# V's second third product between the two banks of scores, the gather in one run, and V's last wide products cut in halves

## The chip, the cores and the metric

The kernel runs on one core of a Trainium2 chip. The metric is the device time of one execution in microseconds (us), the median of several runs. A core has a matrix engine (TensorE, "PE" in the profile, with its weight loads shown apart as "PEld"), a vector engine (DVE), an activation engine (ACT), GpSimd (POOL) and a queue engine for transfers (SP). Matrix products end in PSUM, which has eight banks of 128 x 512 numbers; everything else lies in SBUF.

## The reference, cut to what matters

`x` has 64 graphs of 256 nodes with 512 features; `adj` is 256 x 256 with zeros and ones. Two layers follow each other:

```python
h = relu(layernorm(x))
q, k, v = h @ Wq.T, h @ Wk.T, h @ Wv.T
rel = adj.T * (q @ k.T)                       # scores, per graph
rel = rel / norm(rel, axis=2, keepdims=True)
x = x + rel @ v
h = relu(layernorm(x))
x = x + (adj @ h) @ weight + bias
```

All is float32.

## The kernel before

**Precision by thirds.** A float32 operand is split into three parts, named `u`, `l` and `s` (upper, lower, and one for the cross terms), and a product is the sum of three: u with u, l with l, s with s. Between the second and the third, ACT multiplies the PSUM bank by a constant just over one (line 361). `three` makes these products for one bank: `first(ps)` gives u and l, `second(ps)` the third one. `unit` plans a bank: it takes the next of eight banks, plans `first`, then plans what the unit before has left over in the list `waiting` (its third product and its `drain`), then ACT's multiplication, and puts its own rest into `waiting`. So a unit's third product stands on PE behind the next unit's first two, which hides ACT's multiplication. `finish` plans whatever is in `waiting`.

**Stages.** Two graphs make a pair; there are 32 pairs, numbered from 0. For a pair i, the loop in `pairs` plans:

- `g_stage`: four banks of g = M h, with M = Wq and Wk multiplied once at the start. A third is 4 matmuls of 512 columns (weights `m_*`, moving `h_*` or `hs`). The drain splits g into `gy_u`, `gy_s`, `gy_l` (lines 265, 266, 268).
- `v_stage` for block 0 and for block 1: V = h Wv for 128 nodes each, 4 + 4 + 4 matmuls of 512 columns (tiles `wv_*`, `h_*`, `hs`). The drain writes three rows of `late` (tiles `v_low`, `late_parts`). Block 1's drain is held back in the list `held` until the gather is planned, since it writes over rows that the gather reads.
- `scores`: two banks, one for each graph. A third is 8 matmuls of 256 columns (weights `gy_*`, moving `h_*` or `hs`). The drain multiplies by the adjacency on DVE (line 444) and takes sums of squares on ACT (line 449).
- `gather` of pair i - 1: adj times h of layer 2, four banks of 8 matmuls of 256 columns (weights `late`, moving `adjt_r`). It has no third product, so it plans what is in `waiting` behind its first bank. Its drain splits the result into the same `gy_*` rooms, for `mix` (lines 274 to 276).
- `turn_scores`, `v_stage` for blocks 2 and 3, the turn of the next pair's h (`h_turn`, `h_parts`), `mix` of pair i - 1 (tiles `w_*`, `gy_*`), `attend` of pair i (tiles `v_low`, `late_parts`, `rel_*`), and with its last block `layer_1`, which makes the rows that the next gather reads.

Pair 0 has scores but no gather; in the last pair the gather of that pair follows at the end.

**Order.** The class `Plan` takes the operations with costs and with what they read and write. PE keeps the order in which it was planned. The other engines and queues are ordered by due times, which come from PE's order and from the costs; each engine then runs its list strictly in order. All matmuls are recorded at line 255, in the helper `mm`.

On PE, an ordinary pair around the scores is therefore: V block 0's third product; u and l of the first bank of scores; V block 1's third product; u and l of the second bank; third product of the first bank; first bank of the gather; third product of the second bank; the other three banks of the gather; V blocks 2 and 3.

Of the kernel before, what the change touches and what calls it, by code (L numbers as in the profile page):

```python
# [108 lines left out]
def f(ap):  # L109
    return ap.bitcast(F32)  # L110
# [3 lines left out]
def kernel(  # L114
# [13 lines left out]
    B, N, D = x.shape  # L128
    DC = D // P
    NC = N // P  # L130
# [7 lines left out]
    outs = out.rearrange("(i b) (c p) d -> i p (b c) d", b=NB, p=P)  # L138
# [4 lines left out]
    def room(name, *shape, dtype=F32, tag=None):  # L143
        return pool.tile([P, *shape], dtype, name=name, tag=tag or name)
# [11 lines left out]
    def hp(k, d):  # L156
        return h[k][:, d] if k < 2 else h_s[d // 2][:, d % 2]
# [43 lines left out]
    def late(r):  # L201

        return v_low[:, r] if r < 4 else changing("late", "parts", 8, D, dtype=F32R)[:, r - 4]
# [16 lines left out]
    def by_pe(i):  # L220

        return i < 2 or i + 1 == NP
# [17 lines left out]
    def next_bank(turned=False, on=None):  # L240

        while on is not None and count["bank"] % 8 in in_pieces:
            count["bank"] += 1
        n = count["bank"] % 8
        count["bank"] += 1
        (in_pieces.add if turned else in_pieces.discard)(n)
        return bank[n], ("bank", n)
# [3 lines left out]
    def keys(name, n=DC):  # L251
        return [(name, k) for k in range(n)]

    def mm(out, left, right, first):
        nc.tensor.matmul(out, left, right, start=first, stop=True, skip_group_check=True)  # L255

    MM, HALF = 0.231, 0.1185
# [85 lines left out]
    waiting = []  # L343

    def finish(plan):
        while waiting:
            waiting.pop(0)()

    def unit(plan, first, second, drain, on=None):


        ps, key = next_bank(on=on)
        if on is not None:
            plan.add("ACT", 0.58, lambda: A.copy(ps, on), ["bias"], [key])
        for cost, fn, reads in first(ps):
            plan.add("PE", cost, fn, reads, [key])
        finish(plan)
        if second is None:
            drain(ps, key)
            return  # L360
        plan.add("ACT", 0.49, lambda: A.activation(ps, ps, AF.Copy, scale=ONE), [], [key])  # L361

        def rest():
            for cost, fn, reads in second(ps):
                plan.add("PE", cost, fn, reads, [key])
            drain(ps, key)
        waiting.append(rest)

    def three(left, right, names_l, names_r, cost, outs=None, fresh_bank=True):


        def group(k, ds, begin):
            def first(ps):
                for d in ds:
                    for n, (o, lf, rt) in enumerate(outs(ps, k, d) if outs else [(ps, left(k, d), right(k, d))]):
                        mm(o, lf, rt, begin and d == ds[0] and n == 0)
            return first

        def first(ps):
            for k, ds, begin in ((0, (0, 1), fresh_bank), (0, (2, 3), False), (1, (0, 1, 2, 3), False)):  # L380
                yield cost * len(ds), (lambda go=group(k, ds, begin): go(ps)), [
                    n for d in ds for n in (*names_l(k, d), *names_r(k, d))]

        def second(ps):
            ds = (0, 1, 2, 3)
            yield cost * len(ds), (lambda go=group(2, ds, False): go(ps)), [
                n for d in ds for n in (*names_l(2, d), *names_r(2, d))]
        return first, second

    def named(*names):  # L390
        return lambda k, d: [(names[k], d)]
# [4 lines left out]
    def g_half(b):  # L396

        return lambda k, d: [(name + "uls"[k], d, b) for name in ("gy_", "g_")]
# [4 lines left out]
    h_named = named("h_u", "h_l", "h_s")  # L403
# [12 lines left out]
    def v_stage(plan, i, exact, blocks_of=range(4), hold=False):  # L416
        for c in blocks_of:
            first, second = three(
                lambda k, d, c=c: hp(k, d)[:, ts(c, P)], lambda k, d: wv_p[k][:, d, :],
                h_named, named("wv_u", "wv_l", "wv_s"), MM)  # L420
            rows = [[("late", 3 * c + k)] for k in range(3)]
            if c == 1 and not exact:
                rows[2] = keys("late", 12)[4:]

            def drain(ps, key, c=c, rows=rows):
                split_right_ps(plan, ps, key, [lambda at, k=k: late(3 * c + k) for k in range(3)], rows, None)
            unit(plan, first, second, (lambda ps, key, go=drain: held.append(lambda: go(ps, key))) if hold else drain)

    def scores(plan, i):
        rn = norms[i % 2]  # L430
        for b in range(NB):
            def outs_of(ps, k, d, b=b):
                return [
                    (ps[:, ts(n, N)], g_p[k][:, d, ts(b * NC + n, P)], hp(k, d)[:, ts(b, N)])
                    for n in range(NC)
                ]
            first, second = three(None, None, g_half(b), h_named, 2 * HALF, outs_of)

            def drain(ps, key, b=b):
                dst = plain[:, b].rearrange("p k (t j s) -> p k t j s", t=NC, j=J) if by_pe(i) else rel[:, b]  # L440

                def columns(part):
                    return part.rearrange("p (k t j s) -> p k t j s", k=NC, t=NC, j=J)
                plan.add("DVE", 0.6, lambda: V.tensor_mul(
                    *(part.rearrange("p k t j s -> p (k t) j s") for part in (
                        dst, columns(ps), columns(f(adjt[0]).rearrange("p k m -> p (k m)")))),),
                    [key, "adjt"], [("h_rel", b)])
                for k in range(NC):
                    plan.add("ACT", 0.53, lambda k=k: A.activation(
                        columns(ps)[:, k], dst[:, k], AF.Square, accum_out=rn[:, b, k : k + 1]),  # L450
                        [("h_rel", b)], [key, (f"rn{i % 2}", b, k)])
            unit(plan, first, second, drain)

    def turn_scores(plan, i):
        rn, name = norms[i % 2], f"rn{i % 2}"
# [249 lines left out]
    def pairs(exact):  # L705
        count["bank"] = 4
        waiting.clear()
        rooms.clear()
        plan = Plan()
        turned_adj = room("adjt_r", NC * N + P, dtype=F32R, tag="adjt") if exact else room("adjt", NC * N + P)  # L710
        adjt[:] = [turned_adj[:, P - 16 : P - 16 + NC * N].rearrange("p (c n) -> p c n", c=NC)]
        plan.add("ACT", 0.49, lambda: A.copy(adjt[0].rearrange("p m n -> p (m n)"), bank[6]), [("bank", 6)], ["adjt"])
        first_turn(plan)
        last_m(plan)
        count["bank"] = 4
        turn_wv(plan)
        h_rows(plan, 1)
        h_place(plan, 25.0)
        load(plan, 2)
        first_g(plan)  # L720
        v_stage(plan, 0, exact, (0, 1))
        scores(plan, 0)
        v_stage(plan, 0, exact, (2, 3))
        turn_scores(plan, 0)
        finish(plan)
        h_turn(plan)
        h_parts(plan)
        split_w(plan)
        plan.add("ACT", 0.58, lambda: A.activation(bias_bc, bias_bc, AF.Copy, scale=1.0 / ONE), [], ["bias"])
        attend(plan, 0, exact)  # L730
        for i in range(1, NP):
            last = i + 1 == NP
            load(plan, i, name=f"x{i % 2}")
            if not last:
                h_rows(plan, i + 1)
                h_place(plan)
            if i + 2 < NP:
                load(plan, i + 2)
            g_stage(plan, i)
            v_stage(plan, i, exact, (0,))  # L740
            v_stage(plan, i, exact, (1,), hold=True)
            scores(plan, i)
            gather(plan, i - 1, exact)
            while held:
                held.pop(0)()
            if by_pe(i):
                turn_scores(plan, i)
            v_stage(plan, i, exact, (2, 3))
            if not last:
                if not by_pe(i):  # L750
                    turn_scores(plan, i)
                waiting.append(lambda: (h_turn(plan), h_parts(plan)))
                mix(plan, i - 1)
            attend(plan, i, exact)
            if last:
                mix(plan, i - 1)
                gather(plan, i, exact)
            store(plan, i - 1)
        mix(plan, NP - 1)
        finish(plan)  # L760
        with tc.manual_schedule(engines=in_order):
            plan.run()
# [33 lines left out]
```

## Time and profile before

| What | Value |
| --- | --- |
| Median of 3 runs (lowest, highest) | 1561.76 us (1561.21, 1562.63) |
| The profiled execution's own time | 1560.76 us |
| Its span in the profile | 1559.0 us |
| PE, weight loads, DVE, ACT busy | 99%, 85%, 87%, 66% |
| Granted TensorE clock | 0.999 |
| Matmuls recorded | 8046 |
| Moved from and to HBM | 67 GB/s over the span |

The span is the time from the first to the last instruction of the profiled execution; its own time has 1.8 us more around it. A row of the timeline gives the start, the time until the end of the last one, engine, line, operation, the tiles as out<-in, the shape and how many instructions were merged. Matmuls overlap in it, so the pace of a run is read from the start of one row to the start of the next.

### The profile page before, as it was taken

To read this page: it belongs to the slowest core of one execution; us is meant where nothing else is said; L and a number is where in the kernel's file an instruction comes from. 1 tells how busy PE (TensorE), PEld (TensorE's weight loads), DVE (VectorE), ACT (ScalarE), POOL (GpSimd) and SP (SyncE) were. 2 spreads that over 40 slices of the span, in tenths; PEclk is the share of its full clock that TensorE was granted. 3 is DMA by queue.
4 is the path that set the end of the run, shared out by engine and by line. 5 is a ranking of instruction groups with operands and counts; after the bars stand their busy time and mean duration, and the time that the engine had idled before them with its cause. 6 is when DMAs were issued, how large, how long until landed. Compare 5 with 4: busy or idle time off the path is not lost.

```text
span 1559.0 us, 22543 instructions
## 1 busy us (share of the span) xinstructions
PE 1548.2 (99%) x8046; PEld 1323.5 (85%) x8046; DVE 1355.3 (87%) x2419; ACT 1022.7 (66%) x1941; POOL 24.3 (2%) x39
## 2 busy tenths in 40 slices
PE   9999999999999999999999999999999999999998
PEld 6788888888888888888888888888888888888886
DVE  6997889898889988898988899888989888989786
ACT  5567666666667676666676675766666766666654
POOL 0000000000000000000000000000000000000000
PEclk9999999999999999999999999999999999999999
DMA  5321333223333223333233332233332233322211
GB/s 199 112 83 41 122 111 120 77 71 110 118 113 119 66 78 117 114 117 90 72 96 118 112 122 68 77 114 114 116 106 71 81 121 111 120 71 76 85 55 56
DMA packets 91112, 153.63 MB, mean 99 GB/s; under 512 B 17136, under 2 KB 32240, under 8 KB 90992
## 3 DMA queue, kind: packets, MB, share of 16 engines
q1 hardware_dynamic: 80768, 116.46, 24.7%
q0 software_dynamic: 8432, 32.51, 5.7%
q10 hardware_dynamic: 1792, 3.15, 0.6%
q8 instruction: 65, 1.06, 0.3%
q14 instruction: 55, 0.45, 0.1%
HBM read 70.78 MB, written 33.55 MB: 67 GB/s over the span
## 4 chain that ended last, share of the span: by engine, by line
PE 95%; DVE 3%; DMA 1%; ACT 0%; issue 0%; ACTq 0%; DVEq 0%
PE bank L255 95%; DMA bias_bc<-in_L_gnn_bias_dram 1%; DMA x_ring<-in_x_dram 1%; DVE late_parts L266 0%; DVE late_parts L268 0%; DVE rel_s_parts L470 0%; DVE st L292 0%; DVE rel_l L475 0%; DVE gy_l L275 0%; DVE m_l L268 0%; DVE gy_l L268 0%; DVE wv_l L268 0%; DVE ht L322 0%; DVE wv_s L266 0%; DVE m_s L266 0%
## 5 line engine op out<-in xcount | busy, mean ns | idle before, releaser
L361 ACT ACTIVATE bank<-bank 128x512 f32<-128x512 f32 x572 | 333.5, 583 | 307.8 <-PE bank L255 304.2
L255 PE MATMUL bank<-wv_s,hs 128*128 128x512 f32 x512 | 137.8, 391 | 0.0
L255 PE MATMUL bank<-wv_u,h_u 128*128 128x512 f32 x512 | 137.5, 390 | 0.0
L255 PE MATMUL bank<-wv_l,h_l 128*128 128x512 f32 x512 | 136.9, 389 | 0.0
L255 PE MATMUL bank<-w_u,gy_u 128*128 128x512 f32 x512 | 136.9, 389 | 0.0
L255 PE MATMUL bank<-w_l,gy_l 128*128 128x512 f32 x512 | 136.9, 389 | 0.0
L255 PE MATMUL bank<-h_l,m_l 128*128 128x512 f32 x512 | 136.6, 389 | 0.1
L255 PE MATMUL bank<-w_s,gy_s 128*128 128x512 f32 x512 | 136.7, 389 | 0.0
L255 PE MATMUL bank<-h_u,m_u 128*128 128x512 f32 x512 | 136.5, 389 | 0.0
L255 PE MATMUL bank<-hs,m_s 128*128 128x512 f32 x512 | 136.4, 389 | 0.0
L266 DVE SCALAR_TENSOR_TENSOR gy_s<-gy_u,bank 128x512 fp32r<-128x512 f32 x128 | 86.2, 675 | 43.0 <-ACT gy_u L265 43.0
L255 PEld LDWEIGHTS bank<-h_l,m_l 128*128 128x128 f32 x512 | 96.0, 188 | 20.4 <-DVE h_l L339 0.5
L255 PEld LDWEIGHTS bank<-wv_l,h_l 128*128 128x128 f32 x512 | 96.1, 188 | 20.2
L255 PEld LDWEIGHTS bank<-h_u,m_u 128*128 128x128 f32 x512 | 96.0, 188 | 20.2 <-ACT m_u L265 0.2
L255 PEld LDWEIGHTS bank<-w_l,gy_l 128*128 128x128 f32 x512 | 96.1, 188 | 20.0
L255 PEld LDWEIGHTS bank<-hs,m_s 128*128 128x128 f32 x512 | 96.1, 188 | 19.9
L255 PEld LDWEIGHTS bank<-w_u,gy_u 128*128 128x128 f32 x512 | 96.0, 188 | 20.0
L255 PEld LDWEIGHTS bank<-w_s,gy_s 128*128 128x128 f32 x512 | 96.0, 188 | 20.0 <-ACT bank L361 0.2
L255 PE MATMUL bank<-adjt_r,late_parts 128*128 128x256 f32 x896 | 112.6, 277 | 0.0
L255 PEld LDWEIGHTS bank<-wv_s,hs 128*128 128x128 f32 x512 | 93.8, 188 | 18.3 <-ACT bank L361 0.7
L255 PEld LDWEIGHTS bank<-wv_u,h_u 128*128 128x128 f32 x512 | 93.7, 188 | 17.7
L255 PEld LDWEIGHTS bank<-adjt_r,late_parts 128*128 128x128 f32 x896 | 107.3, 188 | 0.0
(110 smaller groups left out, 3072.3 us busy)
## 6 DMA issues: line engine op xcount, KB each, us to landing
fresh<-in_x_dram SPq DMA_DIRECT2D x31, 1024.0 KB, 5.7
blocks<-h_rel SPq DMA_DIRECT2D x496, 64.0 KB, 2.0
x_ring<-in_x_dram SPq DMA_DIRECT2D x31, 1024.0 KB, 8.0
out_dram<-x_ring POOLq DMA_DIRECT2D x31, 1024.0 KB, 5.4
h_rel<-h_rel SPq DMA_DIRECT2D x464, 32.0 KB, 1.8
blocks<-in_L_gnn_Wv_dram ACTq DMA_DIRECT2D x1, 1024.0 KB, 11.1
x_ring<-in_L_gnn_weight_dram SPq DMA_DIRECT2D x1, 1024.0 KB, 12.3
out_dram<-x_ring SPq DMA_DIRECT2D x4, 256.0 KB, 2.3
```

The source lines that it names most:

```text
L255: nc.tensor.matmul(out, left, right, start=first, stop=True, skip_group_check=True)
L266: plan.add("DVE", 0.63, lambda: V.scalar_tensor_tensor(s(), f(u()), ONE, ps, op0=ALU.mult, op1=ALU.subtract), [*key, *ku], ks)
L361: plan.add("ACT", 0.49, lambda: A.activation(ps, ps, AF.Copy, scale=ONE), [], [key])
```

## The change

Three things change in the order and shape of PE's work.

1. `three` gets a flag `halve`. With it, the last matmul of the third product (k = 2, d = 3, the last chunk of the contraction) is given as two matmuls of 256 columns with the same weights. `v_stage` sets it for blocks 0 and 1, in every pair.
2. `scores` takes a function `between`. It is called after both banks' units are planned; the loop hands it what `waiting` held, that is V block 1's third product with its drain. Taken out of `waiting`, that product no longer stands behind u and l of the first bank.
3. After `between`, `scores` calls `finish`, so that the second bank's third product is planned at once, and not behind the first bank of the gather.

PE's order in pairs 1 to 31 becomes: V block 0's third product; u and l of the first bank of scores; u and l of the second; third product of the first bank; V block 1's third product; third product of the second bank; all four banks of the gather. Pair 0 calls `scores` without `between`: there only the halves are new, and no `finish` is called. The order of SP's and POOL's transfers stays as it was; on DVE and ACT some operations of a pair change places, by the planner's due times.

```diff
-    def three(left, right, names_l, names_r, cost, outs=None, fresh_bank=True):
+    def three(left, right, names_l, names_r, cost, outs=None, fresh_bank=True, halve=False):
...
                 for d in ds:
-                    for n, (o, lf, rt) in enumerate(outs(ps, k, d) if outs else [(ps, left(k, d), right(k, d))]):
+                    whole = outs(ps, k, d) if outs else [(ps, left(k, d), right(k, d))]
+                    if halve and k == 2 and d == DC - 1:
+                        whole = [(o[:, ts(n, N)], lf, rt[:, ts(n, N)]) for o, lf, rt in whole for n in range(NC)]
+                    for n, (o, lf, rt) in enumerate(whole):
                         mm(o, lf, rt, begin and d == ds[0] and n == 0)
...
-                h_named, named("wv_u", "wv_l", "wv_s"), MM)
+                h_named, named("wv_u", "wv_l", "wv_s"), MM, halve=c < NC)
...
-    def scores(plan, i):
+    def scores(plan, i, between=None):
...
             unit(plan, first, second, drain)
+        if between:
+            between()
+            finish(plan)
...
-            scores(plan, i)
+            scores(plan, i, waiting.pop())
             gather(plan, i - 1, exact)
```

## The prediction

> **What bounds the kernel.** First the page's busy shares, then its chain, then the waits of PE.
>
> ```profile
> PE 1548.2 (99%) x8046; PEld 1323.5 (85%) x8046; DVE 1355.3 (87%) x2419; ACT 1022.7 (66%) x1941; POOL 24.3 (2%) x39
> ...
> PE 95%; DVE 3%; DMA 1%; ACT 0%; issue 0%; ACTq 0%; DVEq 0%
> ```
>
> ```profile
> PE bank L255 <- DVE rel_s_parts L470: 1.2, 1, 1.2
> PE bank L255 <- DMA wk_sb<-in_L_gnn_Wk_dram: 1.1, 1, 1.1
> PE bank L255 <- POOL h_rel L612: 1.0, 1, 1.0
> PE bank L255 <- DVE late_parts L268: 0.7, 1, 0.7
> PE bank L255 <- DVE rel_l L475: 0.6, 1, 0.6
> ```
>
> PE is busy for 99% of the span, the chain that ends last is 95% PE, and all waits of PE listed come to 4.6 us, each happening once (start, first pair, last pair). Its weight loads (PEld) were held for ACT bank L361 six times, 2.9 us in all. In an ordinary pair between, no engine and no transfer holds PE up. So the time is the number of matmuls times their pace, and the view that counts is the PE timeline, read from start to start (rows overlap, so the durations in the second column cannot be added). An ordinary pair:
>
> ```profile
> 174.32 1.07 PE L255 MATMUL bank<-wv_s,hs 128*128 128x512 f32 x4
> 175.23 1.10 PE L255 MATMUL bank<-h_u,gy_u 128*128 128x256 f32 x8
> 176.17 1.11 PE L255 MATMUL bank<-h_l,gy_l 128*128 128x256 f32 x8
> 177.12 1.09 PE L255 MATMUL bank<-wv_s,hs 128*128 128x512 f32 x4
> 178.04 1.11 PE L255 MATMUL bank<-h_u,gy_u 128*128 128x256 f32 x8
> 178.99 1.10 PE L255 MATMUL bank<-h_l,gy_l 128*128 128x256 f32 x8
> 179.93 1.11 PE L255 MATMUL bank<-hs,gy_s 128*128 128x256 f32 x8
> 180.87 0.40 PE L255 MATMUL bank<-adjt_r,v_low 128*128 128x256 f32 x2
> 181.11 0.85 PE L255 MATMUL bank<-adjt_r,late_parts 128*128 128x256 f32 x6
> 181.80 1.10 PE L255 MATMUL bank<-hs,gy_s 128*128 128x256 f32 x8
> 182.74 0.40 PE L255 MATMUL bank<-adjt_r,v_low 128*128 128x256 f32 x2
> 182.98 2.66 PE L255 MATMUL bank<-adjt_r,late_parts 128*128 128x256 f32 x22
> 185.47 1.08 PE L255 MATMUL bank<-wv_u,h_u 128*128 128x512 f32 x4
> ```
>
> Scores (gy) from 178.04 to 180.87: 24 matmuls in 2.83 us, **117.9 ns** each. Gather (adjt_r) from 182.98 to 185.47: 22 in 2.49, **113.2 ns** each, for the same shape. Two products of 512 columns take 2 x 226.7 elsewhere (24 of w between 712.76 and 718.20), so 113.3 is half of a wide one and 117.9 is 4.5 ns too slow. Now an odd pair, in which PE's weight load had been held for 0.19 us by ACT at 126.74:
>
> ```profile
> 129.67 1.09 PE L255 MATMUL bank<-wv_s,hs 128*128 128x512 f32 x4
> 130.60 1.07 PE L255 MATMUL bank<-h_u,gy_u 128*128 128x256 f32 x8
> 131.50 1.07 PE L255 MATMUL bank<-h_l,gy_l 128*128 128x256 f32 x8
> 132.41 1.07 PE L255 MATMUL bank<-hs,gy_s 128*128 128x256 f32 x8
> 133.32 0.40 PE L255 MATMUL bank<-adjt_r,v_low 128*128 128x256 f32 x2
> ```
>
> The same scores: 24 in 2.72 us, 113.3 ns. Then the gather of that pair is slow (135.42 to 138.01: 22 in 2.59, 117.7 ns). So a 256-column run has **two paces**, set by how it is entered and kept through the run; four wide products between do not change it (fast on both sides of 129.67); after slow scores the gather is fast, after fast scores it is slow. The stall at 798.49 switched the scores in the same way. Straight from undisturbed wide products the scores always come in slow. Why is not told by the trace.
>
> **What the Trainium skill says.** "TensorE: Matmul & The Clock Gate", section Back-to-back issue gap: the spacing in a stream of weight loads and matmuls is set by both, and its table gives 262 cycles at 256 columns and 518 at 512. That prices a product cut in two at 6 cycles, an estimate of 2.5 ns at the page's 2.4 GHz; the trace has neither figure (113.3 or 117.9, and 226.7), and its bounds are 0 to 9 ns (2 x 113.3 or 2 x 117.9 less 226.7). "Perfetto Trace Analysis", section Identifying the Most-Contended Engine: matmul busy time misleads, weight-load busy is the better measure; here that is 85%, which agrees that something is left, and the pace above says where. "SBUF — State Buffer", section Who interferes with whom: moving operand and weights have a read port each and PE waits on nobody. No run here shows a cause that contradicts it, but two paces with no wait do exist.
>
> **The change, part by part.** The stretch from the first score to the first wide product after the gather takes 185.47 - 175.23 = 10.24 us (10.24 also at 744.49 to 754.73), in 31 pairs. It holds 48 + 32 narrow matmuls and 4 wide ones: at 113.3 and 226.7 that is 9.97. So **0.27 us per pair** can be won at most: 48 x 4.5 ns = 0.22 in the scores, the rest at the changes of kind.
> - *Halves.* The last wide matmul of V's third product becomes two narrow ones, for blocks 0 and 1 in all 32 pairs: 64 more matmuls and weight loads. Direct price 0 to 9 ns each; I take 5, +0.01 us per pair. Their indirect effect is that the scores are no longer entered straight from a wide product. Trace before shows no such entry; bounds: nothing, or 40 scores (all before the second V third) from 117.9 to 113.3, -0.18 us.
> - *V's third moved.* It now stands after the third products of bank 0 and before those of bank 1. Number and operands are unchanged. In before it costs 178.04 - 177.12 = 0.92 against 0.907, and something alike stays. With its own halved last product it can switch the pace once more. I take it that it does: the last 8 scores slow (8 x 4.5 = 0.04 us that stays), and the gather fast as it is now after slow scores. Bounds: gather unchanged, or 32 x 4.5 = +0.14 us.
> - *Gather in one run.* One entry into it less: 182.74 to 185.47 is 24 matmuls in 2.73 against 2.72, and 180.87 to 181.80 is 8 in 0.93 against 0.907; -0.02 us per pair.
> - *What moves on the other engines.* SP and POOL issue the same DMAs in the same order. Bank 0's scores end about 0.9 us earlier, bank 1's about 1 us, so mask, squares and the later DMA turn start earlier; the first gather ends 0.9 us later, the last where it did. Costed at nothing, with this cover: gy_l for bank 0, last written at 744.27 + 0.69 = 744.96, is read last from 746.1; gy_s, ready at 744.26, would be read from about 748.2 instead of 749.2. V's block 1 leaves PE about 2.7 us later; its DVE work on the bank ran at 753.96, the next V product into that bank comes at 756.34, and one gather part of 0.68 us now goes ahead on DVE: some 1.7 us of slack left after 0.68 of work become 1.0. On ACT its copy must follow the second gather anyway, which ends where it did. Later in the pair DVE does the turn of the scores before h's second half and h_l after rel_s; rel_l, now 0.8 us ahead of its first use (769.81 against 770.62), gets more room, and h_l still ends near 772.2 for a use at 776.96. If a cover went, the late one would be V's bank at 756.34, at tenths of a us per pair.
>
> Sum per pair: -0.18 - 0.02 + 0.02 = -0.18 us, times 31 = -5.6; the first pair, which has scores and no gather, -0.1. The profiled execution took 1560.76 us (span 1559.0 and 1.8 around it), so it would come to 1555.1; the median shown is 1.0 above it: 1556.1.
>
> **The rivals.**
> - *All fast* (8%): scores and gather both near 113.3, up to -0.27 x 31 = -8: 1553.5. For it: both paces exist for both kinds. Against it: in no pair of before were both fast throughout.
> - *One switch only* (12%): the first third switches the scores, the second does not; 48 fast scores (-0.22) and 32 slow gathers (+0.14), with the rest -0.06 to -0.09: 1559 to 1560. For it: this is what the pair at 130.60 looks like.
> - *No switch* (16%): the halves are just two more matmuls, +0.01 to +0.02, and the single run of gather returns 0.02: 1561 to 1562.5. This is also the case that the change does not do what it can do.
> - *The gather turns slow and the scores stay slow* (14%): the switch happens only at the second halved third. 40 scores slow, 8 fast (-0.04), 32 gathers at 117.7 (+0.14), halves and entries 0 to +0.02: +0.10 to +0.14, +3.2 to +4.3 in all: about 1565.5. It decides as soon as fewer than 32 of the 48 scores gain their pace while the gather loses its own. Against it: the first entry changes more than the second, which comes in among narrow runs anyway.
>
> **Numbers.** Likeliest, 50%: 1556.1, its own range 1554.5 to 1557.5. A measurement of this kernel can tell about 0.2%, 3.1 us, from no change: faster means below 1558.6. The likeliest, all fast and a part of one switch: 66% faster. The other part and no switch: 20% within. Slower: 14%. The range runs from all fast to no switch, 1553.3 to 1562.6, and leaves out the slower case and little else.
>
> **What would show it.** Right: eight h_u,gy_u matmuls start to start 0.91 us instead of 0.94, in nearly all pairs; the gather's 32 still 3.63 to 3.66; the stretch 10.06 instead of 10.24; PE's waits unchanged. Wrong: scores at 0.94 still; or a gather run of 3.77; or a new repeated wait of PE for DVE late_parts or ACT bank L361.

## The result, and the profile after

The change makes the kernel slower: 1565.56 us (median of 10 runs, 1564.34 to 1566.6) against 1561.85 (10 runs, 1560.27 to 1562.77). The ratio is 1.0023, with a 95% interval of 1.0014 to 1.0032. The profiled execution took 1565.42 us, its span is 1563.6, so 4.6 us over the span before.

The page's busy shares and the chain of the changed kernel; below them, the waits of PE's weight loads between 100 and 1500 us (in total, times, longest), first of the kernel before, then of the changed one:

```profile
PE 1550.4 (99%) x8110; PEld 1327.3 (85%) x8110; DVE 1359.4 (87%) x2419; ACT 1020.7 (65%) x1941; POOL 24.3 (2%) x39
...
PE 85%; DVE 5%; ACT 3%; SPq 3%; DMA 1%; issue 1%; DVEq 0%; ACTq 0%
```

```profile
PEld bank L255 <- ACT bank L361: 0.7, 3, 0.4
```

```profile
PEld bank L255 <- ACT bank L361: 3.2, 6, 0.8
PEld bank L255 <- DVE late_parts L266: 0.4, 1, 0.4
```

PE has the 64 matmuls more, and the chain leaves PE for 15% of the span instead of 5%: something now comes late for PE, which nearly nothing did before. But first the PE timeline of an ordinary pair (columns as before; the row of five wv_s is three wide matmuls and the two halves):

```profile
744.73 1.08 PE L255 MATMUL bank<-wv_s,hs 128*128 128x512 f32 x5
745.64 1.11 PE L255 MATMUL bank<-h_u,gy_u 128*128 128x256 f32 x8
746.59 1.10 PE L255 MATMUL bank<-h_l,gy_l 128*128 128x256 f32 x8
747.53 1.11 PE L255 MATMUL bank<-h_u,gy_u 128*128 128x256 f32 x8
748.47 1.10 PE L255 MATMUL bank<-h_l,gy_l 128*128 128x256 f32 x8
749.41 1.11 PE L255 MATMUL bank<-hs,gy_s 128*128 128x256 f32 x8
750.36 1.09 PE L255 MATMUL bank<-wv_s,hs 128*128 128x512 f32 x5
751.29 1.07 PE L255 MATMUL bank<-hs,gy_s 128*128 128x256 f32 x8
752.20 0.40 PE L255 MATMUL bank<-adjt_r,v_low 128*128 128x256 f32 x2
752.43 0.87 PE L255 MATMUL bank<-adjt_r,late_parts 128*128 128x256 f32 x6
753.14 0.40 PE L255 MATMUL bank<-adjt_r,v_low 128*128 128x256 f32 x2
753.38 2.75 PE L255 MATMUL bank<-adjt_r,late_parts 128*128 128x256 f32 x22
755.97 1.09 PE L255 MATMUL bank<-wv_u,h_u 128*128 128x512 f32 x4
```

From 745.64 to 750.36 stand 40 scores in 4.72 us, 118.0 ns each: the cut product at 744.73 switched nothing. From 751.29 to 752.20 stand 8 in 0.91, 113.8 ns: the cut product at 750.36 did switch. And the gather that comes in behind fast scores is slow, 32 in 3.77 us (752.20 to 755.97), 117.8 ns. The stretch is 10.33 us where before had 10.24; read to the ns over the trace's starts it is 10.325 against 10.246 in nearly every pair, and 0.079 x 31 = 2.4 us. The rest of the 4.6 lies in four pairs between 1126 and 1319 us: their periods, from first score to first score, are 48.15, 47.93, 48.40 and 48.09 us, where 47.53 is the rule. That is 2.45 us together; the start and the end give back some tenths. (A fifth long pair, at 793 us with 47.82, is no loss: before has it too, with 47.90.)

So three theories for the experiments. **A**: a cut V product makes a run of narrow matmuls fast only where it stands inside such a run, and the gather behind fast scores is slow. Rival **B**: the new order itself makes the gather slow. **C**, on the rest of the loss: the long pairs begin with a late load of `fresh`. Each time below stands beside that of the kernel before, run again on the same chip.

### The profile page after: what moved, and what is told of

Same layout as the page of the kernel before. It is cut to its first block, busy times and chain, and to the rows that moved or that the text cites. A ratio compares the mean times of both kernels' runs of the same rounds, so it can differ in the third digit from the quotient of the medians.

```text
span 1563.6 us, 22615 instructions
## 1 busy us (share of the span) xinstructions
PE 1550.4 (99%) x8110; PEld 1327.3 (85%) x8110; DVE 1359.4 (87%) x2419; ACT 1020.7 (65%) x1941; POOL 24.3 (2%) x39
## 4 chain that ended last, share of the span: by engine, by line
PE 85%; DVE 5%; ACT 3%; SPq 3%; DMA 1%; issue 1%; DVEq 0%; ACTq 0%
PE bank L255 85%; SPq L231 3%; DMA fresh<-in_x_dram 1%; DVE st L292 1%; ACT h_rel L306 1%; ACT bank L454 0%; ACT bank L354 0%; ACT gy_u L274 0%; DVE h_rel L449 0%; ACT bank L361 0%; DVE ht L322 0%; DVE late_parts L266 0%; DVE gy_l L268 0%; DVE rel_s_raw L492 0%; DVE gy_s L266 0%
## 5 line engine op out<-in xcount | busy, mean ns | idle before, releaser
L361 ACT ACTIVATE bank<-bank 128x512 f32<-128x512 f32 x572 | 332.7, 582 | 349.1 <-PE bank L255 349.1
L255 PE MATMUL bank<-wv_s,hs 128*128 128x512 f32 (+1 forms) x576 | 138.6, 367 | 0.9 <-ACT bank L361 0.8
L275 DVE TENSOR_TENSOR gy_l<-bank,gy_u 128x512 fp32r<-128x512 f32 x128 | 85.2, 685 | 53.7 <-ACT gy_u L274 53.7
L255 PEld LDWEIGHTS bank<-wv_s,hs 128*128 128x128 f32 x576 | 105.5, 188 | 23.2 <-ACT bank L361 3.2
L255 PE MATMUL bank<-adjt_r,late_parts 128*128 128x256 f32 x896 | 116.0, 281 | 0.0
```

Of the source, the lines that this page charges most:

```text
L275: plan.add("DVE", 0.6, lambda: V.tensor_sub(l, ps, f(u)), [key, *ku], kl)
```

## The experiments

**move_only: the order alone, no cut.**

```diff
-                h_named, named("wv_u", "wv_l", "wv_s"), MM, halve=c < NC)
+                h_named, named("wv_u", "wv_l", "wv_s"), MM, halve=False)
```

> The changed order (V block 1's third product between the two banks' third products, the gather in one run), with no product cut in halves. Theory A (a cut product inside a narrow run switches the pace): all 48 scores stay at 117.8 ns, V's four wide ones take about 0.926 us, the gather's 32 start within 0.02 us to run at 113.3; the stretch from the first score to the first wide product after the gather is about 10.23 us (before 10.246, after 10.325), the time 0 to 1 us below before. Rival B (the order itself, a gather straight behind a bank's third product, makes the gather slow): gather at 117.8, stretch 10.32 or more, 2 us or more above before.

The end of the stretch in its PE timeline:

```profile
1037.75 1.11 PE L255 MATMUL bank<-hs,gy_s 128*128 128x256 f32 x8
1038.69 0.40 PE L255 MATMUL bank<-adjt_r,v_low 128*128 128x256 f32 x2
...
1039.84 2.66 PE L255 MATMUL bank<-adjt_r,late_parts 128*128 128x256 f32 x22
1042.33 0.86 PE L255 MATMUL bank<-wv_u,h_u 128*128 128x512 f32 x3
```

Scores slow (0.94 for 8), gather fast: 22 in 2.49, 113.2 ns; the stretch 10.225. That is A's figure, and B falls: the order does not slow the gather. But the time was 1564.27 (21 runs) against 1561.92, ratio 1.0014 (1.0007 to 1.0020), where A expected a gain. In the profile the loss stands in long pairs, six of them by 0.4 to 1.0 us, and in weight loads held by ACT L361 for 4.8 us in 9 waits. The order brings the long pairs, without any cut.

In one of these long pairs a hold of PE at 461.6 us had made the scores fast ahead of V's whole product. What came behind it:

```profile
463.64 1.07 PE L255 MATMUL bank<-hs,gy_s 128*128 128x256 f32 x8
464.55 1.09 PE L255 MATMUL bank<-wv_s,hs 128*128 128x512 f32 x4
465.48 1.11 PE L255 MATMUL bank<-hs,gy_s 128*128 128x256 f32 x8
466.42 0.40 PE L255 MATMUL bank<-adjt_r,v_low 128*128 128x256 f32 x2
```

Eight in 0.91, then eight in 0.94: here the pace fell behind four wide products. In before, at 129.67 us, the scores kept the fast pace behind four wide ones, and the prediction took that one case for the rule.

**halves_only: the order of before, both cuts.**

```diff
-            scores(plan, i, waiting.pop())
+            scores(plan, i)
```

> The order of before, with the last wide product of V's third cut in halves for blocks 0 and 1. Theory A: the first bank's 16 scores slow; behind the cut V product the 16 of the second bank and the 8 third ones fast (113.3 ns); the gather's first 8 slow (117.8), the 8 scores behind them fast, the gather's other 24 slow; stretch 10.22 to 10.26 us, the time within 1 us of before. Rival B (order, not cut): scores at 117.8 and gather at 113.5 as before, plus up to 0.02 us for the cuts: stretch 10.25 to 10.27.

The PE timeline of halves_only:

```profile
1031.34 1.11 PE L255 MATMUL bank<-h_l,gy_l 128*128 128x256 f32 x8
1032.28 1.09 PE L255 MATMUL bank<-wv_s,hs 128*128 128x512 f32 x5
1033.21 1.07 PE L255 MATMUL bank<-h_u,gy_u 128*128 128x256 f32 x8
1034.12 1.07 PE L255 MATMUL bank<-h_l,gy_l 128*128 128x256 f32 x8
1035.03 1.07 PE L255 MATMUL bank<-hs,gy_s 128*128 128x256 f32 x8
...
1038.04 2.75 PE L255 MATMUL bank<-adjt_r,late_parts 128*128 128x256 f32 x22
1040.63 0.63 PE L255 MATMUL bank<-wv_u,h_u 128*128 128x512 f32 x2
```

Here the reader sees the switch: 0.94 for 8 scores ahead of the cut product, 0.91 for the next 8 behind it and again for the 8 after them, and the gather 22 in 2.59, 117.7 ns. The stretch is 10.236, as A had it; time 1562.91 against 1561.92, ratio 1.0005 (0.9997 to 1.0014). What the cut wins in the scores the gather loses.

**cut_second and cut_first: the changed kernel with one cut each.**

```diff
-                h_named, named("wv_u", "wv_l", "wv_s"), MM, halve=c < NC)
+                h_named, named("wv_u", "wv_l", "wv_s"), MM, halve=c == 1)
```

> The changed kernel with only block 1's product cut, block 0's whole. Theory A with the cut at block 0 idle: the same as the changed kernel in every run of the stretch, 10.31 to 10.325 us, gather at 117.8 ns, 2.5 to 4 us above before. Rival (both cuts are needed): gather at 113.5, stretch about 10.23.

```diff
-                h_named, named("wv_u", "wv_l", "wv_s"), MM, halve=c < NC)
+                h_named, named("wv_u", "wv_l", "wv_s"), MM, halve=c == 0)
```

> The changed kernel with only block 0's product cut, block 1's whole. Theory A: scores slow, gather fast, as with no cut at all but for 0 to 0.01 us: stretch 10.23 to 10.24, time 0 to 1 us below before. Rival (the cut before the first score carries over to the gather): gather at 117.8, stretch 10.32.

With the second cut alone the stretch is 10.325 and the time 1565.29 (ratio 1.0022, 1.0014 to 1.0031): the changed kernel again. With the first alone it is 10.226, as with no cut; the time 1563.77 (1.0012, 1.0004 to 1.0020) is above what was expected, and its profile has long pairs as move_only's has. So the slow gather comes from the second cut alone, and the first one is idle.

**early_cut: block 0's cut product inside the scores.** Is the first cut idle because of the block, or because it stands straight behind wide products? V block 0's third product goes behind the first 8 scores.

```diff
             first, second = three(None, None, g_half(b), h_named, 2 * HALF, outs_of)
+            if early and not b:
+                def first(ps, whole=first):
+                    for n, group in enumerate(whole(ps)):
+                        if n == 2:
+                            early()
+                        yield group
...
             v_stage(plan, i, exact, (0,))
+            early = waiting.pop()
             v_stage(plan, i, exact, (1,), hold=True)
-            scores(plan, i, waiting.pop())
+            scores(plan, i, waiting.pop(), early)
```

> The changed kernel with V block 0's cut third product moved behind the first 8 score matmuls, so that it too stands inside a narrow run. Theory A (a cut V product inside a slow narrow run makes what follows fast): 8 scores at 117.8, then 32 at 113.3. At the second cut V product two cases: it switches back (8 scores slow, gather fast: stretch with both V products 0.11 to 0.13 us shorter per pair than the same work in before, 3 to 4 us, less the long pairs), or a fast run stays fast across it (last 8 scores fast, gather at 117.8: about equal to before, 1561 to 1563). Rival (only block 1's product can switch): 40 scores slow as in the changed kernel, 1565.

The PE timeline of early_cut:

```profile
1028.72 1.11 PE L255 MATMUL bank<-h_u,gy_u 128*128 128x256 f32 x8
1029.66 1.09 PE L255 MATMUL bank<-wv_s,hs 128*128 128x512 f32 x5
1030.59 1.07 PE L255 MATMUL bank<-h_l,gy_l 128*128 128x256 f32 x8
1031.50 1.07 PE L255 MATMUL bank<-h_u,gy_u 128*128 128x256 f32 x8
...
1034.22 1.09 PE L255 MATMUL bank<-wv_s,hs 128*128 128x512 f32 x5
1035.15 1.07 PE L255 MATMUL bank<-hs,gy_s 128*128 128x256 f32 x8
1036.06 0.40 PE L255 MATMUL bank<-adjt_r,v_low 128*128 128x256 f32 x2
...
1037.24 2.75 PE L255 MATMUL bank<-adjt_r,late_parts 128*128 128x256 f32 x22
1039.83 1.09 PE L255 MATMUL bank<-wv_u,h_u 128*128 128x512 f32 x4
```

The same instructions that were idle at 744.73 now switch: 8 scores in 0.94, the next 8 in 0.91. And the second cut does not switch back: 0.91 behind 1035.15, the gather 22 in 2.59. That is the second of the two cases expected. Time 1561.59 against 1561.05, ratio 1.0005 (0.9996 to 1.0013).

It is so in all pairs with a gather but one. In that one, at 127.12 us, PE was held for 0.1 us just ahead of the last score before the first cut product, and the scores behind it were slow. What it is in a cut product that switches, its two narrow matmuls or only that it has five matmuls and weight loads instead of four, no run separates. A plain change of pace at every cut product is ruled out, since the second one leaves fast scores fast.

**pool_after, pool_before, pool_move: the load of `fresh` on POOL's queue**, in the changed kernel, in the kernel before, and in the new order without cuts.

```diff
         dst = fresh if name == "fresh" else ring[i % 2]
+        if name == "fresh":
+            plan.add("POOL", 0.8, lambda: G.dma_start(out=dst, in_=xs[i]), [], keys(name, TC), lands=5.5)
+            return
```

> The changed kernel with the load of the tile fresh issued from POOL's queue, free at that time, instead of SP's behind 16 small transfers. Theory C (part of the loss is pairs that run 0.3 to 0.9 us long, because fresh lands late, DVE's statistics on it push back the order on DVE and ACT, and ACT's multiplication of a V bank, with 0.4 us to spare, comes late for PE): no pair over 47.6 us except the first and the one at about 800 us, 1 to 2.5 us less than the changed kernel, so 1563.0 to 1564.4. Rival (the long pairs have nothing to do with that load): long pairs as before, 1564.3 to 1566.6. The gather stays at 117.8 ns in both.

> The kernel before with the load of fresh on POOL's queue, as a control. Theory C: before has few long pairs to lose, so 0 to 1 us faster. Rival (POOL's queue is simply better or worse for this load): a change as large as in the changed kernel, 1 us or more.

> The changed order with no product cut (as move_only), with the load of fresh on POOL's queue. Theory C (the order costs nothing on PE itself; what move_only lost, it lost in long pairs that begin with a late fresh): no long pair behind the third, gather at 113.4, stretch 10.225, so 0.02 us per pair less than before with POOL's queue: 1559.3 to 1560.3, 4 to 5 us below move_only. Rival (the order itself makes DVE and ACT too late for PE, whenever fresh lands): long pairs stay, 1562 or more.

The waits of PE's weight loads between 100 and 1500 us in move_only (first fence) and in pool_move (second; line 361 is 364 there):

```profile
PEld bank L255 <- ACT bank L361: 4.8, 9, 0.8
PEld bank L255 <- DVE late_parts L266: 0.8, 2, 0.5
```

```profile
PEld bank L255 <- ACT bank L364: 0.7, 2, 0.5
```

No long pair is left behind the third in any of the three. pool_move took 1560.09 (ratio to before 0.9990, 0.9984 to 0.9997): 1.4 us below the before beside it, where move_only was 2.4 above its own. pool_before took 1560.29 (0.9995, 0.9986 to 1.0003) and pool_after 1563.00 (1.0012, 1.0005 to 1.0018), 2.7 us apart, near the 2.4 us of the slow gather. The four long pairs of the changed kernel are also just those in which DVE waited for `fresh` (the one at 793 us left aside), five of the six in move_only had such a wait, and in the three runs with POOL's queue there is none. So C holds: what the order itself loses stands in the long pairs, and nearly all of them begin with a late `fresh`. The new queue does more than bring `fresh` in time, though: the planner then also orders DVE and ACT differently (between 140 and 1500 us DVE's wait for ACT ahead of `gy_s` falls from 40.0 to 2.8 us), so these three runs do not show the landing alone to be the cure.

How the delay reaches PE, in the changed kernel. An ordinary pair, one row of its ACT timeline:

```profile
758.63 0.56 ACT L361 ACTIVATE bank<-bank 128x512 f32<-128x512 f32 x1
```

and one of its PE timeline:

```profile
759.62 1.07 PE L255 MATMUL bank<-wv_s,hs 128*128 128x512 f32 x4
```

Then a long pair; a row of its DVE timeline, with the idle time ahead of it and what ended that:

```profile
1172.39 0.70 DVE L292 BATCH_NORM_STATS2 st<-fresh 128x6 f32<-128x512 f32 x1 [0.51 <-DMA fresh<-in_x_dram]
```

of its ACT timeline:

```profile
1187.92 0.57 ACT L361 ACTIVATE bank<-bank 128x512 f32<-128x512 f32 x1
```

and of its PE timeline:

```profile
1187.37 1.07 PE L255 MATMUL bank<-wv_l,h_l 128*128 128x512 f32 x4
1188.54 1.20 PE L255 MATMUL bank<-wv_s,hs 128*128 128x512 f32 x4
```

Ordinarily ACT ends at 759.19, 0.43 us ahead of V block 2's third product. In the long pair DVE has stood 0.51 us for `fresh`, everything behind it on DVE and ACT is later, ACT ends at 1188.49, and PE's product starts 1.17 us behind the one before instead of 0.91. In before DVE also waited for `fresh` in four pairs (1.7 us in all, 3.0 after), and only one of them was long. What a wait costs in the order of before can be read from halves_only, whose order that is. A row of its DVE timeline:

```profile
743.36 0.69 DVE L292 BATCH_NORM_STATS2 st<-fresh 128x6 f32<-128x512 f32 x1 [0.51 <-DMA fresh<-in_x_dram]
```

The same wait of 0.51 us made that pair 0.10 us longer, and the pair above 0.40. In the five pairs of halves_only that waited 0.5 us or more, 0.40 to 0.42 us of the wait did not reach PE; in the four of the changed kernel it was 0.11 to 0.14. So the new order took some 0.3 us of slack. It is not in the last step: in before, ACT's multiplication ended 0.51 us ahead of PE's product (757.87 against 758.38), little more than the 0.43 of now. What DVE had more of in before was idle time ahead of the two masks of the scores, 0.37 and 1.25 us, now 0.21 and 0.39. That this idle time is the slack that is missing is read from two timelines, not shown by a run of its own.

**adj_shift and late_shift: where the operands lie.** In the first, the gather's moving operand starts 64 bytes later:

```diff
-        adjt[:] = [turned_adj[:, P - 16 : P - 16 + NC * N].rearrange("p (c n) -> p c n", c=NC)]
+        adjt[:] = [turned_adj[:, P : P + NC * N].rearrange("p (c n) -> p c n", c=NC)]
```

> The changed kernel with the gather's moving operand (adjt_r) starting 64 bytes later in its room, nothing else. Theory D (the pace depends on how weights and moving operand lie against each other in SBUF, and the gather lies the other way round from the scores): the gather now keeps the fast pace in which the last 8 scores leave it, 113.3 instead of 117.8 ns, stretch 10.325 - 0.14 = 10.18 us, 4 us less than the changed kernel. Rival (the place in SBUF does not matter, only the order does): gather at 117.8, stretch 10.325, 1565.

The gather in its PE timeline:

```profile
1041.40 2.80 PE L255 MATMUL bank<-adjt_r,late_parts 128*128 128x256 f32 x22
1044.04 0.63 PE L255 MATMUL bank<-wv_u,h_u 128*128 128x512 f32 x2
```

A miss in its sign: 22 in 2.64, 120 ns, slower still than the 117.8 of the changed kernel; 1566.41 us, ratio 1.0036 (1.0023 to 1.0049). The place does change the pace, so the rival falls too. The second adds the early cut, POOL's queue and block 1's product whole, and shifts the gather's weights:

```diff
-    v_low = room("v_low", 4, D, dtype=F32R)
+    v_low = room("v_low", 4 * D + 32, dtype=F32R)[:, 16 : 16 + 4 * D].rearrange("p (r d) -> p r d", r=4)
...
-        return v_low[:, r] if r < 4 else changing("late", "parts", 8, D, dtype=F32R)[:, r - 4]
+        return v_low[:, r] if r < 4 else changing("late", "parts", 8 * D + 32, dtype=F32R)[:, 16 + (r - 4) * D : 16 + (r - 3) * D]
```

> POOL's queue for fresh; V block 0's third product cut and behind the first 8 scores (as early_cut), block 1's whole; the gather's weights (tiles v_low, late_parts) start 64 bytes into their rooms and its moving operand at 0, so that weights and moving operand lie to each other as in the scores. Theory D: a gather that lies as the scores do keeps the scores' pace: 8 scores at 117.8, then 40 scores and all 32 gathers at 113.3, with no steps of 120 at the entry; both V products cost 0.02 us each; stretch from the first score to the first wide product after the gather 10.95 to 10.98 us, where before has 11.15 for the same work; 5 to 6.5 us below before with POOL's queue, 1553.8 to 1555.3. Rival (the gather's pace is always the opposite of the scores', whatever the places): gather at 117 or more, stretch 11.10 or more, 1559 to 1561.

1573.91 us, ratio 1.0080 (1.0063 to 1.0097), a plain miss. Its edit moved more than was meant: every room behind `v_low` lies 128 bytes further, among them `hs` and `gy`. Four wide products of g with `hs` now take 0.92 us (1026.12 to 1027.04 in its PE timeline) instead of 0.907, and the scores stay slow behind the cut. v_behind, which follows and has the same queue and the same cut but the rooms as they were, keeps 0.907. So the pace hangs on the places of rooms, and of more than the gather's; the rule for it is not settled here.

**in_gather and v_behind: what would let both be fast.** Both have the early cut and POOL's queue. In the first, block 1's cut product stands behind the gather's first bank; in the second it is whole and stands between the last scores and the gather.

```diff
-            scores(plan, i, waiting.pop(), early)
-            gather(plan, i - 1, exact)
+            inner = waiting.pop()
+            scores(plan, i, early=early)
+            gather(plan, i - 1, exact, inner)
...
                 unit(plan, first, None, drain)
+                if inner and not b and not d0:
+                    inner()
```

> POOL's queue for fresh; block 0's cut product behind the first 8 scores; block 1's cut product inside the gather, behind its first bank. Theory A leaves two cases. A cut product makes whatever runs slow run fast: the gather's first 8 slow, the other 24 fast, stretch 11.00, 4 to 5 us below before. Or a cut product always leaves the one state in which scores are fast and gathers slow: all 32 gathers at 117.8, stretch 11.10 to 11.13, within 1.5 us of before with POOL's queue.

```diff
         if between:
-            between()
             finish(plan)
+            between()
```

> POOL's queue for fresh; block 0's cut product behind the first 8 scores; block 1's third product whole, between the last scores and the gather. Theory A (four wide products do not make a run forget): after fast scores the gather is slow even behind V's product: 117.8, stretch about 11.11, 1559 to 1560.5. Rival (a gather entered from wide products is fast whatever ran before): gather at 113.5, stretch 10.97, 5 us below before.

The PE timeline of v_behind:

```profile
1028.48 1.07 PE L255 MATMUL bank<-h_l,gy_l 128*128 128x256 f32 x8
1029.39 1.07 PE L255 MATMUL bank<-h_u,gy_u 128*128 128x256 f32 x8
...
1031.21 2.05 PE L255 MATMUL bank<-hs,gy_s 128*128 128x256 f32 x16
1033.09 1.09 PE L255 MATMUL bank<-wv_s,hs 128*128 128x512 f32 x4
...
1035.17 2.66 PE L255 MATMUL bank<-adjt_r,late_parts 128*128 128x256 f32 x22
1037.66 0.63 PE L255 MATMUL bank<-wv_u,h_u 128*128 128x512 f32 x2
```

Both are faster than both kernels: v_behind 1557.48 us (11 runs) against 1561.40, ratio 0.9976 (0.9967 to 0.9985); in_gather 1557.73 (0.9977, 0.9968 to 0.9985). Scores at 0.91 for 8, gather 22 in 2.49. But neither tested what was asked. The 16 third products take 1.88 us: read one by one, 8 fast, a step of 150 ns, 7 slow. The second bank's third product now stands straight behind the first bank's, and ACT's multiplication of that bank ended (1031.99) just as it was due. The step of 150 ns is 36 longer than those ahead of it, and behind it the run is slow; that it was ACT that held PE there is read from these times. So the last 8 scores were slow and the gather fast, as in before. Whether the fast pace survives four wide products on the way into the gather stays open; on the way into scores it did in one pair (before, 129.67) and did not in another (move_only, 464.55). v_behind is 3.9 us below the before beside it, where POOL's queue alone gave 0.8.

## Why the prediction was wrong

**What bounds the kernel** held: PE's pace, with two paces in narrow runs, kept through a run and opposite between scores and gather.

**The halves, first block** is the step that failed. I took 40 scores to go to 113.3, -0.18 us per pair; they stayed at 118.0, so 0. Its reason was that an entry straight from wide products is always slow and that two narrow ones ahead would change it. The trace before could not show that, and early_cut shows what does matter: the same cut product switches where narrow matmuls run ahead of it, not behind wide ones.

**V's third moved**: I took the second cut to switch from fast to slow. It found slow scores and made them fast (0.91 for 8 instead of 0.94); early_cut shows that it leaves fast scores fast. So the last 8 gained 8 x 4.5 = 0.04 us instead of losing it, and the gather lost 32 x 4.5 = 0.14.

**The small terms** were near: the two cuts cost 0.91 - 0.907 and 0.93 against 0.92; the single entry into the gather returned 0.04 rather than 0.02, since fast scores lead into a slow gather with no steps above 120. The 2.5 ns drawn from the skill's table price the gap of a single matmul and not of a stream with weight loads, but the 5 ns that I took came from the trace's bounds. Of the +0.02 in my sum, 0.01 were the halves and 0.01 stand under no part.

Summed: -0.04 + 0.14 - 0.04 + 0.01 = +0.07, by the trace +0.079 us per pair.

**The other engines**, costed at nothing, is the second failed step. I checked covers in an ordinary pair, that of V's PSUM bank on DVE above all, and such a pair does lose nothing. I didn't ask what delay the order can still take up when a load is late: some 0.12 us where it had been 0.4. Line 361 on ACT for V's block 2, which I had not named as a cover, then comes late for PE; I did name its wait as a sign of being wrong, and it came. In the profile this is 2.45 us, in the medians about 1 us (3.7 less the 2.7 between pool_after and pool_before).

**The rivals**: the slower one (+3.2 to +4.3, about 1565.5) is what happened on PE, switch at the second cut included, though part of its sum was filled by the long pairs. What I held against it, that the first entry changes more than the second, is the wrong way round. It had 14%, and the range stopped below it.

## What to carry to other kernels

Where one engine is busy for 99% and waits for nothing, read its pace from start to start by kind of run; a pace can have two values that no wait explains, and what enters a run decides. Before reckoning on a switch, look for the same entry in the trace, with the same kind of work ahead of it: a perturbation inside a run is not one at its door. And a step that is free on the engine that bounds can still spend the slack of the others: count the idle time that it takes away ahead of each strict queue, and what a late load would then cost, not only the due times of an ordinary round.

## What the runs showed of the hardware

- The same 256-column matmul with its weight load runs at 113.3 or 117.8 ns, and in the gather at 120 instead of 117.8 once its moving operand lay 64 bytes further (adj_shift); two such runs behind each other can hold opposite paces. A V product of three wide and two narrow matmuls inside slow scores made the rest fast in every pair in which no hold of PE stood beside it, as long as the rooms lay as in before. Four wide ones never did without a hold; in one pair (move_only, 464.55) they made fast scores slow.
- Behind a single step 36 ns longer than its neighbours the rest of a run of scores kept the other pace (v_behind, 150 ns instead of 114).
- "SBUF — State Buffer" in the Trainium skill, section Who interferes with whom, says that PE waits on nobody and reads both operands through ports of their own. In adj_shift the gather's pace changed from 117.8 to 120 ns with the place of one operand in SBUF and no other edit, so here PE's time depends on where an operand lies; whether the two reads meet is not shown.
- With one load of 1 MB on a free queue instead of behind 16 small transfers, and the order on DVE and ACT that the planner gave with it, the long pairs of the changed kernel were gone; the kernel before became 0.76 us faster by it, which its interval does not tell from nothing.
